# Attention layer 0: which engine reads which score bank, one mask add for three tiles, and the maxima cut into three bf16 parts before they are transposed

## The chip, the cores and the metric

One core of one Trainium2 chip runs the whole program. The metric is device time in microseconds (us) of one execution. Engines by their names in the profile: PE (matmul; PEld is its weight load), DVE (vector), ACT (scalar), POOL (GpSimd) and SP, whose queue issues DMAs. Each engine takes its instructions in order.

## The reference

Five layers follow one another: a grouped-query cross attention (layer 0), an RWKV block, a second attention, its feed-forward, and another RWKV block. The change is in layer 0 alone, which computes, for 16 batches of 100 rows against 361 context rows:

```python
q = hidden_state @ Wq + bq
k = encoder_hidden_state @ Wk + bk
v = encoder_hidden_state @ Wv + bv
...
scores = jnp.einsum('bkgld,bksd->bkgls', q, k) * scale
scores = scores + encoder_attention_mask[:, :, None, :, :]
attn = jax.nn.softmax(scores, axis=-1)
out = jnp.einsum('bkgls,bksd->bkgld', attn, v)
out = out.transpose(0, 3, 1, 2, 4).reshape(b, l, H)
out = out @ Wo + bo
x = out + hidden_state
mu = jnp.mean(x, axis=-1, keepdims=True)
var = jnp.var(x, axis=-1, keepdims=True)
return (x - mu) * jax.lax.rsqrt(var + EPS) * gamma + beta
```

There are 8 key heads of 16 channels, and 4 query heads for each.

## The kernel before, in words

Layer 0 is `layer0` (L352). Its loop (L699) goes over 32 halves `h`: batch `b = h // 2`, and `par = h % 2` says which 4 of the 8 key heads. I call a half with `par` 1 odd, one with `par` 0 even. The work of a half is set in seven slots by `order` (L698): m0, m1, w0, m2, w1, m3, w2. An "m" slot computes **maxima** (L482) of the half that comes next, a "w" slot **weights** (L526) of the present one.

- `maxima(h, q)`: four matmuls, one per head, each on 32 rows of PE, write scores (100 rows x 361 keys) into four PSUM banks; DVE adds the mask and reduces each bank to one column of `nms`, which holds minus the maximum of each row. After the fourth group (m3) DVE copies these columns twice beside themselves (L499).
- `turn_maxima(h)` (L501), at the end of slot 0: PE transposes `nms` into one bank; ACT copies it as bf16 (`high`). At slot 1 `part()` goes on: DVE forms `rest` (rows of the maxima less `high`), ACT the bf16 `mid` of it, POOL adds both into the bf16 tile `parted`. So `parted` holds three bf16 parts of each maximum, in three neighbouring rows.
- `weights(fill, h, j, slot)`: for one of three key blocks of 121 keys, four matmuls make turned scores (121 keys x 400) in four banks (r = 0 to 3), and four bf16 matmuls with `both` add the three parts of the maxima to them. Then the banks are emptied into `pt`: for j = 0, ACT copies r = 0, 1 and DVE adds the mask into r = 2, 3 as it reads them; for j = 1, 2, ACT copies three and DVE reads r = 3. POOL adds the mask to each tile that ACT copied, one instruction for each. The exponentials are put off: the tiles of DVE one slot, those of ACT `far` slots (2, 3, 3).

Score banks come from one ring of six (`score`, L356), handed out in turn: a group takes four, the transposes one. The matmuls of a group run in the order r = 3, 2, 1, 0 (`BURST`, L28). A group therefore starts with the banks that the group before it had as its second and first.

Between these, PE does **filler pieces** (`Filler`, L103): queries, keys, values, `attend` (L567, the product with the values; three per half), `divide` (L596) and `output` (L619, four pieces `o`). Each piece has a cost and a first slot. In each slot the filler gets a share, a ninth of the cost of all pieces in the list, and takes the first piece in the list that may run, until the share is spent; what is left or overdrawn goes on to the next slot. Pieces of one chain stay together, and after a chain is closed no other chain starts in that slot. The attends of a half are due at slots 5, 8 and 10, where 7 and more are slots of the next half. `divide` of a batch is due in slot 5 of the next batch's even half; its result is `s`, DVE takes reciprocals, and in slot 4 of the odd half POOL multiplies `y` by them, after which the four `o` pieces go to the end of the list, due from slot 5. Batches 0, 4 and 8 have two queries pieces to place in the odd half, batches 1, 2, 5, 6, 9 and 10 one, the others none. After `o` come DVE's residual `res`, statistics (POOL `ve`, `rstd`), then POOL `shift`, ACT `res` and POOL's last two products.

All helpers record as L89 (vector, scalar, gpsimd), L94 (matmul) or L97 (transpose), so groups are told apart by tiles. PE's order is the order of the program.

## Time and profile before

| what | value |
|---|---|
| median of 3 runs | 3151.25 us (3147.79 to 3153.27) |
| the profiled execution | 3151.7 us, span 3149.8 us |
| granted PE clock, mean | 0.960 |
| layer 0, in the span | from 0 to about 698.6 us |
| busy from 30 to 620 us (590 us) | PE 499.9, DVE 397.9, POOL 369.5, ACT 345.0 |
| the same, a batch without queries (576.2 to 613.9) | PE 32.0, DVE 26.8, POOL 26.0, ACT 23.4 of 37.7 |
| POOL mask add, 121x400 | 256 times, mean 1034 ns |
| ACT copy of a score bank, 121x400 | 256 times, mean 499 ns |
| DVE maxima reduce, 100x361 | 512 times, mean 533 ns |
| DVE mask add, 121x400 | 560 ns |
| DVE `rest`, ACT `mid`, POOL `parted`, 128x400 | 626, 628, 942 ns |

The times come from runs without the profiler; the span is what the profiler saw of one execution, from first to last instruction. In a timeline line the columns are start in us, duration in us, engine, source line, operation, written tile and read tiles, shape, count; in brackets the idle time of the engine just before, and what ended it. A float32 matmul counts as two instructions there. A matmul's end is modelled, so PE's busy time is an upper view of its work.

### The profile page before, as it was taken

The page shows a single profiled execution, that of the slowest core. Times are in us where ns is not written, and L with a number is a line of the kernel's source. Part 1 is how long each engine was busy: PE and PEld are TensorE (multiplying, and loading weights), DVE is VectorE, ACT ScalarE, POOL GpSimd, SP SyncE. Part 2 cuts the span into 40 slices and gives each one's busy share as a digit, 9 for nine tenths or more (in the row PEclk, how much of TensorE's full clock was granted, in tenths as well). Part 3 has the DMA queues.
Part 4 walks back from the last instruction along what each step waited for, and adds up shares of the span by engine and source line. Part 5 has one row for each costly group of instructions (what it writes and reads, how often), then busy time and mean ns, then how long its engine had stood idle before and what let it go on. Part 6 is the DMA issues. An engine that isn't in the chain of part 4 may idle for free. (4 is left out here: it accounts for less than half of the span.)

```text
span 3149.8 us, 43449 instructions
## 1 busy us (share of the span) xinstructions
PE 2819.1 (89%) x16083; PEld 1375.6 (44%) x16083; DVE 1752.6 (56%) x3603; ACT 1237.6 (39%) x2249; POOL 1491.1 (47%) x1291
## 2 busy tenths in 40 slices
PE   6888888858889999989999999989999788989998
PEld 3333333314344444445454555445554344444444
DVE  4676767742989989523434333331000379898981
ACT  2565566643344355422223232221111335344553
POOL 1666666663777777512222111130000367777871
PEclk9999999979899999989999999999999889999999
DMA  6010101004224253130000001020002223324321
GB/s 195 15 43 14 36 21 37 10 19 123 70 80 133 83 162 108 52 106 21 20 21 21 21 21 34 28 70 11 11 11 60 96 69 110 102 76 150 109 61 56
DMA packets 139559, 195.90 MB, mean 62 GB/s; under 512 B 23974, under 2 KB 106854, under 8 KB 139346
## 3 DMA queue, kind: packets, MB, share of 16 engines
q1 hardware_dynamic: 116306, 160.34, 17.1%
q10 hardware_dynamic: 23040, 32.78, 2.9%
q8 instruction: 127, 2.08, 0.3%
q14 instruction: 86, 0.70, 0.1%
HBM read 117.16 MB, written 49.15 MB: 53 GB/s over the span
## 5 line engine op out<-in xcount | busy, mean ns | idle before, releaser
L89 POOL TENSOR_TENSOR a<-a,rc 128x800 f32<-128x800 f32 x256 | 487.5, 1907 | 180.5 <-DVE a L89 124.7
L89 DVE TENSOR_TENSOR_SCAN a<-wc,vb 128x400 f32<-128x400 f32 x512 | 477.4, 974 | 29.4 <-PE acc L94 3.2
L89 DVE CUSTOM_DVE_ANT_0 l_junk<-l_sc,mask 100x361 f32<-100x361 f32 x512 | 273.1, 533 | 163.2 <-PE l_sc L94 104.9
L89 POOL TENSOR_TENSOR pt<-pt,maskT 121x400 f32<-121x400 f32 x256 | 258.0, 1034 | 117.4 <-ACT pt L89 117.4
L89 DVE TENSOR_TENSOR vb<-vb,kc 128x792 f32<-128x792 f32 x256 | 253.8, 991 | 8.8
L1690 DVE CUSTOM_DVE_ANT_0 junk<-l2a_sc,mask 100x361 f32<-100x361 f32 x256 | 136.9, 535 | 182.6 <-PE l2a_sc L94 164.3
L1726 POOL TENSOR_TENSOR pa<-pt,pt 121x1600 f32<-121x1600 f32 x16 | 57.1, 3570 | 364.1 <-ACT pt L1721 364.1
L94 PE MATMUL vb<-xc,sel 128*128 128x400 f32 x512 | 206.9, 487 | 20.3 <-DVE a L89 20.1
L89 POOL TENSOR_TENSOR xj<-tm,ext 128x400 f32<-128x400 f32 x160 | 153.6, 981 | 79.8 <-DVE tm L89 68.3
L1911 DVE TENSOR_TENSOR x<-pb,x 100x512 f32<-100x512 f32 x16 | 12.6, 790 | 320.1 <-DMA pb<-po 310.8
L94 PE MATMUL v<-l_v_w,ct 128*121 128x512 f32 x384 | 177.2, 605 | 0.0
L75 PE MATMUL h<-yTb,l_fc 128*128 128x400 f32 x512 | 172.8, 499 | 0.6 <-ACT yTb L343 0.6
L94 PE MATMUL k<-ct,l_k_w 128*128 128x361 f32 x512 | 170.6, 476 | 0.0
L75 PE MATMUL p<-l_proj,h 128*128 128x512 f32 x384 | 165.4, 592 | 0.0
L89 ACT ACTIVATE pt<-pt 121x400 f32<-121x400 f32 (+1 forms) x192 | 160.1, 880 | 1.0 <-POOL pt L89 0.8
L89 ACT COPY pt<-l_sc 121x400 f32<-121x400 f32 x256 | 110.4, 499 | 108.9 <-PE l_sc L94 108.9
L94 PEld LDWEIGHTS vb<-xc,sel 128*128 128x128 f32 x512 | 97.1, 198 | 113.0 <-DVE a L89 38.1
L94 PE MATMUL l_sc<-kz,qz 32*100 32x361 f32 x1024 | 112.2, 507 | 32.1 <-DVE nms L89 27.1
L75 PEld LDWEIGHTS h<-yTb,l_fc 128*128 128x128 f32 x512 | 96.9, 190 | 74.3 <-ACT yTb L343 2.5
L1721 ACT ACTIVATE pt<-l2a_sc,kmask 121x400 f32<-121x400 f32 x192 | 98.2, 594 | 65.4 <-PE l2a_sc L94 65.4
L94 PEld LDWEIGHTS k<-ct,l_k_w 128*128 128x128 f32 x512 | 93.2, 189 | 64.0 <-issue 14.5
L89 ACT ACT_TABLE_LOAD x66 | 84.7, 1283 | 91.3 <-PE mm L94 65.7
(324 smaller groups left out, 5310.6 us busy)
## 6 DMA issues: line engine op xcount, KB each, us to landing
ct<-in_ctxT SPq DMA_DIRECT2D x32, 722.0 KB
dk<-k ACTq DMA_DIRECT2D x32, 200.0 KB
kc<-dk SPq DMA_DIRECT2D x32, 200.0 KB
dv<-v ACTq DMA_DIRECT2D x32, 200.0 KB
dhi<-hi ACTq DMA_DIRECT2D x32, 200.0 KB
dlo<-lo SPq DMA_DIRECT2D x32, 200.0 KB
vc<-dv SPq DMA_DIRECT2D x32, 200.0 KB
dw<-wd ACTq DMA_DIRECT2D x32, 200.0 KB
```

Source lines behind the costliest of these rows:

```text
L75: nc.tensor.matmul(out=ps, lhsT=lhs(c), rhs=rhs(c), start=(c == 0), stop=(c == n - 1))
L89: return lambda *args, **kw: tc.keep_in_program_order(op(*args, **kw))
L94: pin(nc.tensor.matmul(**kw))
L1690: nc.vector.tensor_tensor_reduce(out=junk, in0=ss[r][:L, :S2], in1=t["mask"], scale=-1.0, scalar=FLT_MAX, op0=ALU.add, op1=ALU.min, accum_ ...
L1721: nc.scalar.activation(pt[:, r, :], st[r][:KW, :T], AF.Exp, bias=t["kmask"][:, j : j + 1], scale=1.0)
L1726: nc.gpsimd.tensor_tensor(t["pa"], t["pt"][0], pt, ALU.add)
L1911: nc.vector.tensor_tensor(x, pb[:, i, :], x, ALU.add)
```

## The change

In `layer0`:

- `weights`: for every j DVE adds the mask as it reads bank r = 0, ACT copies r = 1, 2, 3, and POOL adds the mask to these three tiles in one instruction of 121x1200. The exponential of DVE's tile is put off one slot, that of the three tiles three slots.
- the attend of j = 0 is due at slot 6 in place of 5.
- the maxima are cut into bf16 parts on POOL, right after m3's reduces and before the transposes: twice a copy into the bf16 tile `cut`, a subtraction into the next column, and a copy back, six instructions on 100x16 elements. `turn_maxima` is then four transposes and one ACT copy into `parted`; `part()`, with `rest`, `mid` and POOL's add, is gone, as are the two column copies on DVE.
- in the setup, `both` is built by one reduce per parity, and `less01` and `low01` are gone.

```diff
--- before.py
+++ after.py
@@ -365,19 +365,15 @@
             rows = one.tile([L, 3, E], F32, name="l0_rows")
 
             par01 = one.tile([128, 2], F32, name="l0_par")
-            less01 = one.tile([128, 2], F32, name="l0_less")
-            low01 = one.tile([128, 2], F32, name="l0_low")
             both = one.tile([128, 2, KW], BF16, name="l0_both")
-            mv0 = one.tile([128, 2], F32, name="l0_pair")
+            mv0 = one.tile([128, 1], F32, name="l0_three")
             bqs = one.tile([128, 4], F32, name="l0_bqs")
             kb = one.tile([128, 2], F32, name="l0_kb")
             swap = one.tile([128, 128], F32, name="l0_swap")
             junk = one.tile([L, S2], F32, name="l0_junk")
             vzs = [one.tile([KW, 3, 2, 128], F32, name=f"vz{i}") for i in range(2)]
             nms = [one.tile([L, 4, 128], F32, name=f"nms{i}") for i in range(2)]
-            high = one.tile([128, T], BF16, name="l0_high")
-            mid = one.tile([128, T], BF16, name="l0_mid")
-            rest = one.tile([128, T], F32, name="l0_rest")
+            cut = one.tile([L, 4, 4], BF16, name="l0_cut")
             parted = [one.tile([128, T], BF16, name=f"parted{i}") for i in range(2)]
 
             live, qzs, xTs = {}, {}, {}
@@ -496,7 +492,10 @@
                     )
                 if q == 3:
                     n = nms[par].rearrange("p q (r two s) -> p two s q r", two=2, s=16)[:, 1 - par]
-                    vector.tensor_copy(n[:, 1:3], n[:, 0:1].to_broadcast([L, 2, 4, 4]))
+                    for k in range(2):
+                        gpsimd.tensor_copy(cut, n[:, k])
+                        gpsimd.tensor_tensor(n[:, k + 1], n[:, k], cut, ALU.subtract)
+                        gpsimd.tensor_copy(n[:, k], cut)
 
             def turn_maxima(h):
 
@@ -504,16 +503,7 @@
                 ps = score()
                 for q in range(4):
                     turn(ps[:, q * L : (q + 1) * L], nms[par][:, q, :], ident[:L, :L])
-                scalar.copy(high, ps[:, :T])
-
-                def part():
-                    vector.scalar_tensor_tensor(
-                        rest, high, less01[:, par : par + 1], ps[:, :T], ALU.mult, ALU.add
-                    )
-                    scalar.activation(mid, rest, AF.Identity, scale=low01[:, par : par + 1])
-                    gpsimd.tensor_tensor(parted[par], rest, mid, ALU.add)
-
-                return part
+                scalar.copy(parted[par], ps[:, :T])
 
             def turn_mask(b):
                 ps = score()
@@ -541,28 +531,23 @@
                     start=False,
                 )
                 pt = t["pt", par]
-                far = (2, 3, 3)[j]
-
-                def masked(engine, dst, src, n):
-                    m = t["maskT"][:, j, None, :].to_broadcast([KW, 4 * n, L])
-                    engine.tensor_tensor(dst, src, m, ALU.add)
-
-                def parts(ap):
-                    return ap.rearrange("p (q t) -> p q t", t=L)
-
-                for r in range(far):
+                m = t["maskT"][:, j, :]
+                vector.tensor_tensor(
+                    pt[:, j, 0, :].rearrange("p (q t) -> p q t", t=L),
+                    ss[0][:KW, :T].rearrange("p (q t) -> p q t", t=L),
+                    m[:, None, :].to_broadcast([KW, 4, L]), ALU.add,
+                )
+                for r in range(1, 4):
                     scalar.copy(pt[:, j, r, :], ss[r][:KW, :T])
-                for r in range(far, 4):
-                    masked(vector, parts(pt[:, j, r, :]), parts(ss[r][:KW, :T]), 1)
-                for r in range(far):
-                    masked(gpsimd, parts(pt[:, j, r, :]), parts(pt[:, j, r, :]), 1)
+                three = pt[:, j, 1:4, :].rearrange("p r (q t) -> p (r q) t", t=L)
+                gpsimd.tensor_tensor(three, three, m[:, None, :].to_broadcast([KW, 12, L]), ALU.add)
 
                 def exp(lo, hi):
                     e = pt[:, j, lo:hi, :].rearrange("p r t -> p (r t)")
                     scalar.activation(e, e, AF.Exp)
 
-                fill.later.append((slot + 1, lambda: exp(far, 4)))
-                fill.later.append((slot + far, lambda: exp(0, far)))
+                fill.later.append((slot + 1, lambda: exp(0, 1)))
+                fill.later.append((slot + 3, lambda: exp(1, 4)))
 
             def attend(fill, b, par, j, slot):
                 n = KEYS[j][1]
@@ -662,17 +647,10 @@
             vector.tensor_reduce(par01, h8, AX.X, ALU.add)
             vector.tensor_scalar(bqs, bq, 0.25, None, ALU.mult)
             vector.tensor_scalar(kb, par01, bk, None, ALU.mult)
-            first = ident.rearrange("p (r two s) -> p two s r", two=2, s=16)
+            starts = ident.rearrange("p (r two s) -> p two s r", two=2, s=16)
             for par in range(2):
-                less, low, pair = less01[:, par : par + 1], low01[:, par : par + 1], mv0[:, par : par + 1]
-                vector.tensor_reduce(pair, first[:, 1 - par, 0, :], AX.X, ALU.add)
-                vector.tensor_reduce(less, first[:, 1 - par, 1, :], AX.X, ALU.add)
-                vector.tensor_reduce(low, first[:, 1 - par, 2, :], AX.X, ALU.add)
-                vector.tensor_tensor(less, less, low, ALU.add)
-                vector.tensor_tensor(pair, pair, less, ALU.add)
-                vector.tensor_copy(both[:, par, :], pair.to_broadcast([128, KW]))
-            vector.tensor_scalar(less01, less01, -1.0, None, ALU.mult)
-            vector.tensor_scalar(low01, low01, -1.0, None, ALU.mult)
+                vector.tensor_reduce(mv0, starts[:, 1 - par, 0:3, :], AX.XY, ALU.add)
+                vector.tensor_copy(both[:, par, :], mv0.to_broadcast([128, KW]))
             halves = ident.rearrange("p (r two s) -> p two r s", two=2, s=16)
             turned = swap.rearrange("p (r two s) -> p two r s", two=2, s=16)
             for par in range(2):
@@ -704,7 +682,7 @@
                     elif b + 1 < B:
                         values(fill, b + 1)
                     if h > 0:
-                        for j, slot in enumerate((5, 8, 10)):
+                        for j, slot in enumerate((6, 8, 10)):
                             attend(fill, b, 1, j, slot)
                         divide(fill, b, 12)
                     if h > 0 and b % G < 3 and b // G + 1 < NG:
@@ -719,20 +697,18 @@
                         gpsimd.tensor_tensor(xb[b], xb[b], rows[:, 0, :], ALU.add)
                     if b + 1 < B:
                         keys(fill, b + 1)
-                    for j, slot in enumerate((5, 8, 10)):
+                    for j, slot in enumerate((6, 8, 10)):
                         attend(fill, b, 0, j, slot)
                 share = fill.total() / 9
                 due = 0.0
                 for slot, (what, i) in enumerate(order):
-                    if slot == 1 and h >= 0:
-                        part()
                     if what == "m" and h + 1 < 2 * B:
                         maxima(h + 1, i)
                     if what == "w" and h >= 0:
                         weights(fill, h, i, slot)
                     due = fill.run(slot, due + share)
                     if slot == 0 and h >= 0:
-                        part = turn_maxima(h)
+                        turn_maxima(h)
                     if slot == 3 and par and b + 1 < B:
                         turn_mask(b + 1)
                 fill.carry(7)
```

## Prediction

> **What bounds the kernel now.** The change touches only the first of five layers, so I first ask how long that layer runs and whether its end is waited for. The slices of the page (78.7 us each) are coarse; the timeline around 690 us gives the hand-over:

> ```profile
> 697.37 1.26 POOL L89 TENSOR_TENSOR x<-res,l_rows 100x512 f32<-100x512 f32 x1
> 698.66 1.52 ACT L89 ACTIVATE xn_a<-x,fshift,frstd 100x512 f32<-100x512 f32 x2 [2.72 <-POOL x L89]
> 698.66 1.00 DVE L89 TENSOR_SCALAR xn_a<-x,fmv,frstd 100x512 f32<-100x512 f32 x2 [5.10 <-POOL x L89]
> ```

> The last line of layer 0 is POOL's `x`, and ACT and DVE of the next layer start at 698.66, when it ends. So a microsecond in layer 0 is a microsecond of the span. Inside the layer the waits of the matmul engine (PE) from 30 to 651 us are read (total us, times, longest):

> ```profile
> PE l_sc L94 <- DVE nms L89: 49.4, 60, 3.2
> PE acc L94 <- ACT pt L89: 16.9, 49, 0.6
> PE k L94 <- DVE res L89: 11.5, 13, 1.2
> PE l_sc L94 <- ACT pt L89: 2.8, 6, 1.0
> PE o L94 <- POOL y L89: 2.0, 6, 0.3
> ```

> PE is busy 499.9 of the 590 us from 30 to 620, DVE 397.9, POOL 369.5, ACT 345.0. PE runs its hand-written order, and what it loses are short waits for a PSUM bank or a tile. One row speaks to the first part of the change: PE waited for ACT to empty a score bank for 2.8 us in all. Then the order of PE's work in the half that begins at 577.50 (batch 13, a batch without `queries` pieces), from its last maxima (slot 5) to the next half's first, and POOL beside it:

> ```profile
> 592.05 0.87 PE L94 MATMUL l_sc<-kz,qz 32*100 32x361 f32 x8
> 593.21 0.88 PE L94 MATMUL acc<-pt,vz 121*32 121x400 f32 x8 [0.29 <-ACT pt L89]
> 594.29 0.95 PE L94 MATMUL l_sc<-qz,kz 32*121 32x400 f32 x8 [0.20 <-DVE nms L89]
> 595.06 0.35 PE L94 MATMUL l_sc<-parted,l_both 32*121 32x400 bf16 x4
> 595.74 1.10 PE L94 MATMUL o<-l_wo,y 128*100 128x512 f32 x2 [0.33 <-POOL y L89]
> 596.77 0.87 PE L94 MATMUL l_sc<-kz,qz 32*100 32x361 f32 x8
> ...
> 591.68 3.02 POOL L89 TENSOR_TENSOR pt<-pt,maskT 121x400 f32<-121x400 f32 x3 [2.88 <-ACT pt L89]
> 594.65 1.03 POOL L89 TENSOR_TENSOR y<-y,s 128x400 f32<-128x400 f32 x1
> 596.05 3.01 POOL L89 TENSOR_TENSOR pt<-pt,maskT 121x400 f32<-121x400 f32 x3 [0.36 <-ACT pt L89]
> ```

> Reader's point: the first output piece `o` already waits 0.33 us for POOL's `y`, though an attend (`acc`) and a weights group stand before it.

> **The change, part by part.** The sum is made against the profiled execution: 3151.7 us, span 3149.8; the median shown is 3151.25, so the two agree to 0.5 us.

> (a) *Work counts.* ACT: 32 more copies (w0 now copies three banks; 499 ns each) and 32 `mid` fewer (628 ns): nothing net. DVE: 32 masked adds (560), 32 `rest` (626) and 32 small copies (211) fewer, some 45 us of a queue that is not full. POOL: 32 `parted` (942) fewer; 96 merged masks in place of 256 single ones; 192 split instructions more. No row has a 1200-wide POOL add: between 800 (1907 ns) and 1600 (3570) it comes to 2.74 us, against 3.0 for three singles. No row has the split either (100x16): the nearest are COPY 128x16, 211 ns, TENSOR_TENSOR 100x4, 201, and the start-to-start distance of two dependent small ones, 0.28 (`shift` at 579.14 and 579.42). Six at 0.28 make 1.7 us; bounds are 6 x 0.2 = 1.2 and, if each took half of the 100x512 form, 6 x 0.63 = 3.8. I take 1.7, the rows nearest in width. No DMA moves. The setup loses a few 0.15 us DVE instructions beside the first key projections: nothing.

> (b) *Bank one to DVE.* A group's first two banks are wanted by the next group but PE waits for ACT there 2.8 us in all, nearly all of it in the first batch, which has no output pieces between its groups. Worth 1 us (bounds 0 and 2.8).

> (c) *`rest` leaves DVE.* In the even half PE's w0 waits for DVE (0.74 us at 602.22), because `rest` (600.50 to 601.05) holds back the reduces of the maxima before. Without it the second reduce ends as long after its matmuls' start as at 604.35, where w1 follows at 606.45: 2.10 us. From 599.80 that is 601.90: a gain of 0.32 per batch, 15 batches, 4.8 us. It is at most 0.74 x 15 = 11.

> (d) *The split stands in POOL's queue ahead of w2's mask.* It waits for the last reduce and takes 1.7 us. Behind it are the mask, then `shift`, then ACT's `res`, and behind `res` on ACT the exponentials that PE's next attend wants:

> ```profile
> 576.16 3.02 POOL L89 TENSOR_TENSOR pt<-pt,maskT 121x400 f32<-121x400 f32 x3 [0.28 <-ACT pt L89]
> 579.14 0.19 POOL L89 TENSOR_TENSOR shift<-mv,rstd 100x1 f32<-100x1 f32 x1
> 579.67 0.81 ACT L89 ACTIVATE res<-res,shift,rstd 100x512 f32<-100x512 f32 x1 [2.80 <-POOL shift L89]
> 580.39 1.61 ACT L89 ACTIVATE pt<-pt 121x1200 f32<-121x1200 f32 x2
> ```

> The last reduce ends at 575.6; split to 577.5; mask to 580.2; everything after it about 1.0 later. The attend in the odd half's slot 1 goes from 581.73 to 582.7. In a batch without queries the wait of w0 for DVE (0.92 at 622.22) covers it: +0.1. In a batch with queries two or three `v` pieces follow and w0 has no wait (470.29): +1.0. The transposes themselves have cover: PE waits 1.43 us for DVE right after them, so a split of up to some 3.9 us does not show there.

> (e) *Three ACT copies in w0, not two*, put 0.43 us before the exponential that slot 3's attend waits for: 0.43 in odd halves with one query, covered by the waits of w1 elsewhere.

> (f) *The first attend moves from slot 5 to slot 6.* In even halves PE already takes it in slot 6: no change. In odd halves I worked the filler's list by hand. Without queries the pieces are five attends at 0.8, three `v` at 0.9 and a divide at 0.7: 7.4 / 9 = 0.82 a slot; slot 5 has 0.62 left and today takes the attend. Afterwards the attend may not run there, and the only piece that may is the first `o` (due from slot 5). PE then stands behind w1's mask and `y` on POOL. The merged mask begins after the third copy (592.4), ends at 595.2, `y` at 596.2; PE has been free since 593.0. So `o` 596.3 to 597.3, w2 to 598.4, attend to 599.2, and the next maxima at 599.2 in place of 596.77: +2.4. Batches 3, 7, 11, 12, 13 and 14: six.
> With one query (1, 2, 5, 6, 9, 10) slot 5 takes a second query piece, slot 6 the attend and, with 0.03 of its share left, `o`, whose `y` is ready by then. PE's 0.30 wait at the attend goes, one `o` is pulled forward.

> Sum per batch: no query 0.1 + 2.4 - 0.3 = +2.2, six times 13. One query: 1.0 + 0.43 - 0.3 (attend) - 0.3 (c), about +0.7 once the pulled `o` is counted: 4. Two queries (4, 8): 1.0 - 0.3 - 0.3 = +0.4: 1. First batch -1. The tail (from 651 us) loses 0.9 by the attend that now follows the divide of 650.34, gains 0.9 because w0 no longer waits 1.62 for `parted`, and loses 0.6 by the merged masks: +0.6. Total 13 + 4 + 1 - 1 + 0.6 = **+17.6**, so 3151.7 + 17.6, about **3169 us**. Bounds: split 1.2 us, the stall of (f) at 1.7 and (c) at twice its worth give +5; split 3.8 us adds about 2 at the attend in 14 odd halves less the 0.9 that is covered in six: +17.6 + 22 = +40 at the far end.

> [...]

> **The rivals.**
> 1. *The banks were the bound.* If every wait of PE for DVE outside the two fixed ones (1.43 us after the transposes, a chain of three reduces, 14 times: 20 us) went with the lighter DVE queue, 49.4 - 20 = 29 us would go; half of it is a fair price: 3137. For it: the largest wait row names DVE. Against it: after most maxima PE waits for reduces that follow their own matmuls, which no lighter queue shortens.
> 2. *All hidden.* Losses of (d) and (f) are taken up by later waits, as PE idles 5.5 us in each batch without queries: 3151 +/- 5. It holds if the stalled DVE and ACT have work whose results PE wants next; I find none, since after the late maxima every chain starts from PE. That "bank one" does nothing by itself, (b), is the part of this that I believe.
> 3. *POOL is the bound.* If the split takes 3.8 us or POOL's queue runs late all through the half, the attends slip by 2 us more in each odd half: 3185 to 3191. It decides from a split of some 2.5 us on. For: POOL is already 63% busy here; against: the small rows.

> **How the numbers follow.** Forecast 0.73; rival 1 0.08, rival 2 0.09, rival 3 0.10. Time 3169, its own range 3159 to 3179. With rival 3's lower half and most of rival 2: 3153 to 3186. A measurement can tell 0.2% (6 us) from nothing: faster 0.08, same 0.09, slower 0.83.

> **What would show it.** In the profile after: PE `o` waiting for POOL `y` some 3 us in six odd halves, in place of 0.33; the odd half's first `acc` waiting about 1.5 us for ACT, not 0.55; w0 of the even half waiting some 0.4 and not 0.74; six split instructions of 0.2 us on POOL between w1's and w2's masks; one POOL mask of 2.7 us per group. The forecast is wrong if `o` is not ahead of the last weights group in those batches, if `y` no longer stands behind w1's mask, or if the split lasts over 2.5 us.

## The result, and the profile after

| | median us (lowest to highest) | runs |
|---|---|---|
| before | 3149.59 (3147.79 to 3153.27) | 4 |
| after | 3179.89 (3173.02 to 3181.90) | 4 |
| ratio, 95% interval | 1.0091 (1.0072 to 1.0110) | |

The change costs 0.9%: by the interval 23 to 35 us, against 17.6 forecast. The profiled run took 3173.02 us (span 3171.2), the fastest of the four and 21.3 more than that of before. By stages: layer 0 ends at 716.5 instead of 698.6 (+17.9); layer 1, counted up to the first scores of the next layer's attention, takes 6.3 us more; the rest takes 2.7 less (1707.3 against 1710.0).

First the waits of PE in layer 0 after (30 to 680 us; total us, times, longest):

```profile
PE l_sc L94 <- DVE nms L89: 37.6, 42, 3.1
PE o L94 <- POOL y L89: 19.8, 6, 3.3
PE acc L94 <- ACT pt L89: 14.7, 14, 4.1
PE k L94 <- DVE res L89: 7.5, 13, 0.7
PE l_sc L94 <- ACT pt L89: 0.6, 1, 0.6
```

The second row is the new one: six waits of 3.3 us for POOL's `y`, where before had 0.33 or 0.34 in the same six places. The last row shows that PE waits less for ACT to free a bank (2.8 before, 0.6 now). The largest wait, for DVE's `nms`, lost 12 us (49.4 before); not all of that need be the lighter DVE queue, since due5 below, which lacks the six stalls, has 41.8. Here is one of the six, in batch 13's odd half, from the fourth maxima (m3) to the next half's first (PE's timeline after):

```profile
600.49 0.87 PE L94 MATMUL l_sc<-kz,qz 32*100 32x361 f32 x8
604.67 1.26 PE L94 MATMUL o<-l_wo,y 128*100 128x512 f32 x2 [3.31 <-POOL y L89]
605.86 1.71 PE L94 MATMUL l_sc<-qz,kz 32*121 32x400 f32 x8
607.34 0.56 PE L94 MATMUL l_sc<-parted,l_both 32*121 32x400 bf16 x4
607.83 1.38 PE L94 MATMUL acc<-pt,vz 121*32 121x400 f32 x8
609.14 0.87 PE L94 MATMUL l_sc<-kz,qz 32*100 32x361 f32 x8
```

The order is the predicted one: `o` first, then w2, then the attend. But the durations, the second number of a line, are new. The same w2 took 0.95 us before, its `parted` matmuls 0.35 and the attend 0.88; here 1.71, 0.56 and 1.38. The stretches of after around this place, each as long as the shortest piece of half clock (below), tell why (stretch in us, length, busy us of PE, PEld, DVE, ACT, POOL with counts, granted PE clock, DMA share, GB/s):

```profile
598.65:602.07 3.42, 2.71 (x28) 1.39 (x24) 2.67 (x7) 3.28 (x8) 1.19 (x2) 1.00 0.00 0
602.07:605.48 3.41, 0.81 (x2) 0.25 (x2) 1.62 (x6) 0.71 (x2) 3.20 (x6) 1.00 0.00 0
605.48:608.90 3.42, 3.42 (x21) 0.94 (x20) 0.57 (x1) 0.97 (x3) 0.58 (x3) 0.50 0.00 0
608.90:612.31 3.41, 3.41 (x24) 1.46 (x24) 1.93 (x7) 1.87 (x4) 3.02 (x2) 1.00 0.03 7
```

PE is busy for only 0.81 us of the second stretch, at full clock, and the third, with w2 and the attend, is granted half the clock. In all the traces the clock record knows two values, 1.0 and 0.5, and between 60 and 650 us the 0.5 lies in pieces of 3.41 or 6.83 us. After five of the six stalls w2 takes 1.18 to 1.71 us; after the one at 521.8 it keeps its 0.95.

POOL one batch later in after, where `y` is late:

```profile
641.74 2.73 POOL L89 TENSOR_TENSOR pt<-pt,maskT 121x1200 f32<-121x1200 f32 x1 [2.22 <-ACT pt L89]
644.42 1.04 POOL L89 TENSOR_TENSOR y<-y,s 128x400 f32<-128x400 f32 x1
645.39 0.22 POOL L89 CAST l_cut<-nms 100x16 bf16<-100x16 f32 x1
645.69 0.23 POOL L89 TENSOR_TENSOR nms<-nms,l_cut 100x16 f32<-100x16 f32 x1
645.98 0.21 POOL L89 CAST nms<-l_cut 100x16 f32<-100x16 bf16 x1
```

The merged mask lasts 2.73 us (2.74 predicted), the split comes at 0.27 to 0.30 from start to start (0.28 predicted).

### The profile page after: what moved, and what is told of

It is laid out like the page before. It is cut to its first block, busy times and chain, and to the rows that moved or that the text cites. A ratio compares the mean times of both kernels' runs of the same rounds, so it can differ in the third digit from the quotient of the medians.

```text
span 3171.2 us, 43319 instructions
## 1 busy us (share of the span) xinstructions
PE 2851.7 (90%) x16083; PEld 1381.7 (44%) x16083; DVE 1716.1 (54%) x3497; ACT 1231.8 (39%) x2249; POOL 1506.2 (47%) x1291
## 3 DMA queue, kind: packets, MB, share of 16 engines
q1 hardware_dynamic: 116306, 160.34, 17.1%
## 5 line engine op out<-in xcount | busy, mean ns | idle before, releaser
L89 POOL TENSOR_TENSOR a<-a,rc 128x800 f32<-128x800 f32 x256 | 488.2, 1910 | 178.1 <-DVE a L89 116.7
L89 DVE TENSOR_TENSOR_SCAN a<-wc,vb 128x400 f32<-128x400 f32 x512 | 477.2, 973 | 28.1 <-DVE vb L89 2.0
L89 DVE CUSTOM_DVE_ANT_0 l_junk<-l_sc,mask 100x361 f32<-100x361 f32 x512 | 273.8, 535 | 181.0 <-PE l_sc L94 131.7
L89 POOL TENSOR_TENSOR pt<-pt,maskT 121x1200 f32<-121x1200 f32 x96 | 262.7, 2737 | 178.8 <-ACT pt L89 178.8
L89 DVE TENSOR_TENSOR vb<-vb,kc 128x792 f32<-128x792 f32 x256 | 253.7, 991 | 8.8
L94 PE MATMUL vb<-xc,sel 128*128 128x400 f32 x512 | 208.8, 491 | 18.6 <-DVE a L89 18.3
L89 POOL TENSOR_TENSOR xj<-tm,ext 128x400 f32<-128x400 f32 x160 | 154.2, 987 | 84.0 <-DVE tm L89 74.4
L94 PE MATMUL v<-l_v_w,ct 128*121 128x512 f32 x384 | 177.2, 605 | 0.0
L89 ACT COPY pt<-l_sc 121x400 f32<-121x400 f32 x288 | 123.1, 501 | 133.9 <-PE l_sc L94 133.2
L94 PE MATMUL k<-ct,l_k_w 128*128 128x361 f32 x512 | 170.6, 476 | 0.0
L89 ACT ACTIVATE pt<-pt 121x400 f32<-121x400 f32 x192 | 159.1, 884 | 1.3 <-POOL pt L89 1.3
L94 PEld LDWEIGHTS vb<-xc,sel 128*128 128x128 f32 x512 | 97.5, 198 | 110.8 <-issue 39.3
L94 PE MATMUL l_sc<-kz,qz 32*100 32x361 f32 x1024 | 113.2, 510 | 26.4 <-DVE nms L89 25.8
L94 PE MATMUL acc<-pt,vz 121*32 121x400 f32 (+1 forms) x768 | 119.9, 532 | 17.4 <-ACT pt L89 17.4
L94 PEld LDWEIGHTS k<-ct,l_k_w 128*128 128x128 f32 x512 | 93.2, 189 | 64.0 <-issue 14.5
```

Source lines behind the costliest of these rows:

```text
L89: return lambda *args, **kw: tc.keep_in_program_order(op(*args, **kw))
L94: pin(nc.tensor.matmul(**kw))
```

## The experiments

After the result my theory was: the due slot alone is the loss, by its stall and the half clock that follows; the rival: it is the new parts, the merged mask and the split. Later groups ask what each new part costs, and then what the half clock costs. In the table, "L0" is where the last instruction of layer 0 ends in the profiled run, and "half" how many us of half clock lie between 60 and 650 us of that run. Ratios are to the kernel before, on the same chip in the same job; the medians of before in the three jobs were 3153.66, 3155.54 and 3151.36.

| kernel | what it is | median us | ratio (95%) | L0 | half |
|---|---|---|---|---|---|
| before | | 3149.6 | 1 | 698.6 | 17 |
| after | | 3179.9 | 1.0091 (1.0072 to 1.0110) | 716.5 | 24 |
| due5 | after, due slot back at 5 in odd halves | 3157.15 | 1.0008 (0.9998 to 1.0017) | 707.2 | 10 |
| before_due6 | before, due slot 6 in odd halves | 3177.18 | 1.0070 (1.0050 to 1.0090) | 721.8 | 36 |
| warm | after, PE kept at work in the six stalls | 3166.71 | 1.0041 (1.0027 to 1.0055) | 713.5 | 17 |
| due5_dve | due5, split on DVE | 3166.71 | 1.0030 (1.0017 to 1.0043) | 713.1 | 7 |
| after_again | after, once more | 3178.49 | 1.0079 (1.0061 to 1.0096) | 727.7 | 48 |
| weights_only | before, new weights alone | 3162.89 | 1.0022 (1.0013 to 1.0032) | 707.8 | 3 |
| split_pool | before, split alone | 3181.77 | 1.0085 (1.0066 to 1.0104) | 726.6 | 61 |
| split_dve | split_pool, split on DVE | 3183.59 | 1.0091 (1.0070 to 1.0111) | 738.3 | 55 |
| busy_before | before, one idle matmul per odd half | 3150.08 | 1.0000 (0.9987 to 1.0014) | 699.5 | 3 |
| busy_split_pool | split_pool, the same matmul | 3161.81 | 1.0039 (1.0022 to 1.0056) | 716.6 | 37 |
| busy_after | warm, the same matmul | 3163.82 | 1.0042 (1.0021 to 1.0063) | 709.2 | 0 |

(For before_due6 three runs from 3169.83 to 3182.62 are given; a fourth of 11045.86 us isn't in the ratio.)

**The due slot, taken back (due5).**

```diff
-                        for j, slot in enumerate((6, 8, 10)):
+                        for j, slot in enumerate((5, 8, 10)):
```

in the odd half's list alone.

> The changed kernel with the odd half's first attend due at slot 5 again, all else kept. Theory (the six odd halves without queries lose about 3.4 us each, 2.4 by the order and 1 by PE at half clock after the 3.3 us wait): PE's wait of o for POOL y falls from 19.8 us to under 3, layer 0 ends near 697 us in place of 716.5, and the time comes to 3151 +/- 5. Rival (the split on POOL and the third ACT copy are the cost): at least 3165.

The time came as the theory had it: level with before. PE's wait for `y` in layer 0 is down to this row of due5:

```profile
PE o L94 <- POOL y L89: 3.2, 7, 1.1
```

Layer 0 itself ended later than it should have: 8.5 us after before's, of which later layers of that profile gave back 6.4. So the other parts aren't free inside the layer.

**The due slot alone (before_due6).** The same edit the other way round, on before.

> The kernel before with one number changed: the odd half's first attend due at slot 6. Theory: o waits for y some 2.8 us in six odd halves (y ends 0.5 earlier here, with single masks), 1.8 us lost by the order each and up to 1 by the half clock: 3150 + 11 to 17, so 3161 to 3167. Rival (the due slot alone is harmless; it takes the merged masks and the split): 3148 to 3153.

This one number costs 0.7%, more than the theory's own sum. Batch 11's odd half in before_due6 shows the stall without any new mask or split, and the half clock behind it:

```profile
524.95 2.03 PE L94 MATMUL o<-l_wo,y 128*100 128x512 f32 x2 [2.82 <-POOL y L89]
526.91 1.66 PE L94 MATMUL l_sc<-qz,kz 32*121 32x400 f32 x8
```

The stall is 2.82, but `o` takes 2.03 instead of 1.10 and w2 1.66 instead of 0.95: 1.6 us lost behind the wait, on top of it. The odd halves without queries last 23.0 us where the clock holds and 25.0, once 26.0, where it doesn't (before: 19.9 to 21.3). The rival, that the new parts are the loss, falls as a full account.

**The stall kept, the clock held (warm).** In the six halves three matmuls whose result is overwritten stand before the first `o`:

```diff
                     t = bank(f"o0_{b}")
+                    if b + 2 < B and ((b + 1) % G == 3 or b + 1 >= 12):
+                        for _ in range(3):
+                            mm(out=t[:L, :], lhsT=ident[:, :L], rhs=wo[:, 0, :], start=True, stop=True)
```

> The changed kernel with three matmuls of 100x512 that nothing reads, issued in the bank of o while PE waits for y in the six odd halves without queries. Theory (a wait of 3.3 us lets the clock fall, and w2 and the attend after it then run at half speed): w2 after o takes 0.95 us again, not 1.71, and 1.1 us a half is won: layer 0 ends near 710, about 3173 against the changed kernel's 3180. Rival (the slow matmuls have another cause, or the extra ones delay o): layer 0 ends at 716 or later.

Batch 3's odd half in warm:

```profile
201.00 2.82 PE L94 MATMUL o<-l_wo,ident 128*100 128x512 f32 x6
204.35 1.10 PE L94 MATMUL o<-l_wo,y 128*100 128x512 f32 x2 [0.54 <-POOL y L89]
205.38 0.95 PE L94 MATMUL l_sc<-qz,kz 32*121 32x400 f32 x8
206.43 0.88 PE L94 MATMUL acc<-pt,vz 121*32 121x400 f32 x8
```

`o` is as late as in after, but w2 and the attend run at full clock, in all six halves. The ratio falls from 1.0091 and 1.0079 (after, measured twice) to 1.0041, intervals apart: some 12 to 16 us, or 2 to 2.6 for each stall, without `o` coming sooner. The profiled layer 0 ends 3.0 us before the first profile of after and 14.1 before the second; their half clock was 24 and 48 us, against 17 here.

**The split on DVE (due5_dve).** In due5, the six small instructions go from `gpsimd` to `vector`, to see whether POOL's queue is what the split costs.

> As due5, with the six split instructions on DVE in place of POOL. Theory (the split holds up POOL's w2 mask and through shift and ACT's res the next odd half's first attend by 1 us, which shows in the eight odd halves with queries): the first acc's group in these halves ends 1 us sooner, 4 to 8 us won against due5, about 3145. Rival (that delay is hidden, and 1.2 us more on DVE holds banks): equal to due5 or slower.

It was slower, not faster. DVE in due5_dve, and POOL beside it:

```profile
657.76 0.17 DVE L89 CAST l_cut<-nms 100x16 bf16<-100x16 f32 x1
657.97 2.74 DVE L89 TENSOR_TENSOR nms<-nms,l_cut 100x16 f32<-100x16 f32 x1
...
657.95 2.71 POOL L89 TENSOR_TENSOR pt<-pt,maskT 121x1200 f32<-121x1200 f32 x1 [0.70 <-ACT pt L89]
```

A subtraction of 100x16 lasts 2.74 us; POOL's mask began 0.02 us before it and ended 0.05 us before it. This is the one of 64 that lasts so (median 187 ns), but PE then waits 5.10 us for DVE's `res`, and this half lasts 20.96 us in place of due5's 15.36: 5.6 of the 5.9 us by which layer 0 ends later than there. Whether every execution has it isn't known.

**The same kernel again (after_again).**

> The changed kernel as it is, beside the three that follow on one chip. It should repeat 1.007 to 1.011 of the kernel before.

The ratio repeats, but this profile has twice the half clock of the first (48 us, 24) and layer 0 ends 11.2 later. So layer 0's +17.9 in the first profile was the lower of two draws; this one has +29.0.

**The new weights alone (weights_only).** The hunk of `weights` in the change, put on before: banks, merged mask, exponentials; not the due slot, not the split.

> The kernel before with the new emptying of the score banks alone (DVE reads bank one, ACT three, one mask instruction on POOL, exponentials at one and three slots); the maxima's chain and the due slots as before. Theory (bank one is worth nothing, the merged mask that waits for the third copy and the third copy in w0 put 1.0 us on odd halves with queries, nine of them): 3 to 10 us slower than before, layer 0 ends at 702 to 708, odd halves with one query take 22.3 us or more in place of 21.3, even halves the same 17.4. Rival (banks freed sooner are worth something): not slower.

As the theory said. In the odd half's slot 1 the mask on POOL can only start after the third copy, and the attend's last matmuls end 2.9 us after the maxima's start instead of 2.3. PE in weights_only:

```profile
472.98 0.87 PE L94 MATMUL l_sc<-kz,qz 32*100 32x361 f32 x8 [1.32 <-DVE nms L89]
473.77 0.86 PE L94 MATMUL acc<-pt,vz 121*32 121x400 f32 x2
475.02 0.87 PE L94 MATMUL acc<-pt,vz 121*32 121x400 f32 x6 [0.38 <-ACT pt L89]
```

The attend is cut in two: a quarter of it (r = 0, DVE's tile, exponentiated early) runs at once, the rest waits. That breaks PE's idle stretch, and this profile has only 3 us of half clock (17 before).

**The split alone (split_pool, split_dve).** The hunks of `maxima`, `turn_maxima` and the setup on before, with `part()` gone; then with the six instructions on `vector`.

> The kernel before with the maxima split on POOL ahead of the transposes and one ACT copy after them, the emptying of banks and the due slots as before. Theory (rest no longer holds up DVE: 0.3 to 0.5 us an even half, 15 of them; the split in front of w2's masks costs 1 us in the eight odd halves with queries): the even halves take 17.0, the odd with one query 22.3, layer 0 ends within 4 us of 699. Rival (the split on POOL is the costly part): layer 0 ends at 705 or later.

> As split_pool, with the six split instructions on DVE. Theory (nothing stands in front of w2's masks now): even halves 17.0 and odd ones 21.3, layer 0 ends 4 to 8 us sooner than before, about 3145. Rival (DVE's instructions with two inputs in SBUF wait for POOL's masks, as one of 2.74 us did, and hold up the reduces or res): no gain against split_pool.

Both of my sizes for split_pool were far too small: alone, the split costs nearly as much as the whole change. Batch 9's odd half in split_pool:

```profile
441.06 1.32 PE L94 MATMUL l_sc<-kz,qz 32*100 32x361 f32 x8 [1.53 <-DVE nms L89]
443.40 1.56 PE L94 MATMUL acc<-pt,vz 121*32 121x400 f32 x8 [1.02 <-ACT pt L89]
444.88 3.60 PE L94 MATMUL v<-l_wv,ct 128*121 128x128 f32 x16
448.41 0.95 PE L94 MATMUL l_sc<-qz,kz 32*121 32x400 f32 x8
```

The wait for ACT is only 1.02 us, but it follows one of 1.53, and the work after them runs slow: `acc` 1.56 for 0.88, two `v` pieces 3.60 where after has 2.01 for them. 61 of 590 us are at half clock. The even halves are shorter as forecast (mostly 17.1 us, before 17.4); the loss is in the odd ones. On DVE the split is no better: its median copy back is 564 ns instead of some 180. All 75 split instructions that last over 0.3 us there end 0.03 to 0.05 us after a POOL instruction, 70 of them after a mask, as the one of 2.74 us did; and the transposes come later.

**What the half clock costs (the busy three).** One matmul, whose result is overwritten by the transposes, stands ahead of them in odd halves and shortens PE's idle stretch:

```diff
                 ps = score()
+                if par and 0 < h < 2 * B - 1:
+                    mm(out=ps[:, :512], lhsT=ident, rhs=wo[:, 0, :], start=True, stop=True)
```

> The kernel before with the same extra matmul. Theory: its 17 us of half clock go, layer 0 ends at 690 to 694, 4 to 8 us faster than before (ratio 0.997 to 0.999), so faster than both kernels. Rival: the extra work costs PE as much as it saves, same or slower.

> split_pool with one extra matmul of 128x512 that nothing reads, in the transposes' bank ahead of them, in the odd halves, where PE waits 1.5 us for DVE anyway. Theory (split_pool is slow by PE's half clock, which some 60 us of its stretch from 60 to 650 us show against 17 before, each costing 0.4 us; the clock falls where PE idles about half of a 3.4 us window, and the extra matmul breaks that idle stretch): hardly any half clock is left, layer 0 ends at 701 to 707 in place of 726.6, and 20 us or more of the time go. Rival (the split's place in POOL's queue costs the time by itself, the clock only follows): layer 0 ends past 718.

> The changed kernel with that extra matmul and with the three of the run warm. Theory: no half clock is left from 60 to 650 us; what remains is the order alone, layer 0 ends near 706, the time is 10 to 15 us over before (ratio 1.003 to 1.005). Rival: if the order costs less than thought, under 1.002.

In busy_before the half clock goes from 17 to 3 us and the time stays; I was wrong to expect a gain. The two profiles show both sides: batches 2 to 14 take 4.2 us less (501.0 against 505.1), 3.2 of it in batches 6 and 8, which had half clock, but batch 2 begins 5.5 us later. Of these, 2.6 come ahead of the first transposes, where no extra matmul has run yet, and 2.0 in batch 1, which has the remaining piece of half clock. How much of that the extra matmul causes isn't shown. In split_pool the same matmul gains about 14 us (ratio 1.0085 to 1.0039) although it adds work. Layer 0 ends at 716.6, where I expected 701 to 707, since 37 us of half clock are left: the wait of `acc` behind it is untouched.

```profile
475.02 1.13 PE L94 MATMUL l_sc<-l_wo,ident 128*128 128x512 f32 x2
477.11 0.87 PE L94 MATMUL l_sc<-kz,qz 32*100 32x361 f32 x8 [0.62 <-DVE nms L89]
479.46 0.95 PE L94 MATMUL acc<-pt,vz 121*32 121x400 f32 x8 [1.48 <-ACT pt L89]
480.34 3.56 PE L94 MATMUL v<-l_wv,ct 128*121 128x128 f32 x16
```

busy_after has no half clock at all in the 590 us. Beside busy_before it shows what the change costs without it, which the next part uses. No version tried beats before; due5 and busy_before are level with it.

## Why the prediction was right in sign and short in size

*The mechanism of (f) was right.* Six stalls of 3.29 to 3.31 us in the six odd halves named, `o` ahead of w2; taken away (due5), the loss goes, and put alone on before (before_due6), it comes. Rival 3's condition falls (the split takes 1.7 us in after, though without the new weights it was dear all the same: split_pool), rival 2 falls with the result, and so does rival 1: 12 us less waiting for DVE at the scores came with a layer that is 17.9 us longer. Nor were the small steps wrong: w0 of the even half waits 0.46 us (0.4 predicted), and with single masks, in before_due6, the stall is 2.82 and not 3.30, the 0.5 us by which the expectation of before_due6 had `y` end sooner there.

*The size failed at (f)'s price.* The sum's "the next maxima at 599.2 in place of 596.77: +2.4" prices a stall by the wait and the new order alone, and takes every piece behind it at its old duration. The granted clock wasn't in the sum. It could have been: before's own tail has the pattern, 2.79 us of idle and then an attend of 1.56 instead of 0.88 and a w2 of 1.71 instead of 0.95:

```profile
658.08 1.56 PE L94 MATMUL acc<-pt,vz 119*32 119x400 f32 x8 [2.79 <-ACT pt L89]
659.57 1.71 PE L94 MATMUL l_sc<-qz,kz 32*121 32x400 f32 x8
```

Where the clock falls behind such a stall, the half lasts some 1.6 us more: in after 23.1 us where it holds, which is 2.3 over before's 20.8 and so what (f) said, and 24.7 in three halves where it doesn't (27.5 in batch 12's, where it falls twice).

*Without the half clock the sum was some 4 us too high.* Beside each other, busy_before and busy_after give layer 0 +9.7 us (699.5 to 709.2), but their medians differ by 13.7 (3150.08 and 3163.82). The 9.7 is a low draw: busy_after's profiled run is the fastest of its seven, and busy_before's layer 0 began late, with the first transposes at 58.1 us (55.2 to 57.4 in the other profiles). Up to batch 2's transposes busy_after is 5.7 us ahead, where after is 1.8 ahead of before; from there to the end of the layer it takes 15.5 more. So the work costs about 14 us, against 17.6 forecast. By parts of the 9.7, lengths taken from transposes to transposes:

| part | predicted | busy pair |
|---|---|---|
| odd halves, no queries (6) | +2.5 each: 15 | +2.3 each: 13.9 |
| odd halves, one query (6) | about +1.1 each: 6.8 | 6.6 in all |
| odd halves, two queries (2) | +0.7 each: 1.4 | 2.1 |
| even halves (15) | -0.32 each, (c): -4.8 | -13.2, of it -3.0 in batches 0 and 1 |
| up to the first transposes (predicted for the first batch) | -1 | -2.6 |
| tail after the last transposes | +0.6 | +2.9 |

The odd halves without queries are as predicted (batch 0's, which isn't in the table, is 0.1 shorter, and the last even half 0.2 longer). The even halves gain more than (c): -0.3 to -0.4 is the common case, but after a half with one queries piece it is -1.2 to -1.6, because one `o` (1.0 us) has moved out of it into the odd half before, while the prediction counted it at 0.1 net. That makes the agreement of the odd halves with one query luck: the `o` is in their 6.6 us, and without it they lose at most 0.5 each, not 1.1. From such an odd half to the end of the next even one, batches 2 to 10 come to -0.2 or +0.3 us, where the sum has about +0.7. So (d) and (e) were mis-sized there: the first attend does end 0.6 to 1.1 later, but little of that is left at the end of the half; the waits for ACT's `pt` from 30 to 651 us went from 49 (16.9 us) to 13 (10.6). The tail was mis-sized, since (f) acts there too, and twice the wait is longer than before's 2.79 and 2.17. After:

```profile
674.36 1.55 PE L94 MATMUL acc<-pt,vz 119*32 119x400 f32 x6 [4.08 <-ACT pt L89]
683.03 3.73 PE L94 MATMUL o<-l_wo,y 128*100 128x512 f32 x4 [5.15 <-POOL y L89]
```

On top of the work stands the half clock: layer 0 ends 7.3 us later than busy_after's in after's profile (24 us of half clock) and 18.5 in after_again's (48 us), 0.3 to 0.4 us for each; the ratios (1.0091 and 1.0079 beside 1.0042) make it 12 to 15. So a forecast with both right would have been about 14 for the work and 12 to 15 for the clock; mine got as near as it did partly by luck, because too high a work term stood in for some of the clock that it lacked.

*(d) was put down to one part alone.* The odd half's first attend mostly ends 3.4 us after the maxima's start, as predicted (2.3 + 1.0), though with a wait of 0.9 and not 1.5 us, since a quarter of it runs ahead. But the split without the merged mask gives 3.3 and the merged mask without the split 2.9: they overlap, and either alone has most of the effect. The times overlap even more: alone the new weights cost 0.22% and the split 0.85%, together (due5) 0.08%. After, slot 1 of an odd half:

```profile
467.17 0.87 PE L94 MATMUL l_sc<-kz,qz 32*100 32x361 f32 x8 [1.42 <-DVE nms L89]
467.96 0.86 PE L94 MATMUL acc<-pt,vz 121*32 121x400 f32 x2
469.71 0.87 PE L94 MATMUL acc<-pt,vz 121*32 121x400 f32 x6 [0.89 <-ACT pt L89]
470.51 2.01 PE L94 MATMUL v<-l_wv,ct 128*121 128x128 f32 x16
```

DVE's early tile seems to be what protects after here: the split's delay is the same as in split_pool, but `acc` x2 stands in the middle of it and `v` keeps its clock. That early start as the reason for the kept clock is read from the traces; no run put the old banks' order under the new split with nothing else changed.

*Open.* Layer 1, counted as above, lasts 741.2 us in before's profile and 747.4 to 747.6 in after, after_again and warm, but 741.3 in busy_after, though its instructions are the same in all of them; over all profiles it goes from 741.0 to 747.6, and the last layer, from its first `xn_a`, from 692.6 to 703.4. What sets this wasn't tried, and 6 us of the measured loss may lie there.

## What to carry to other kernels

Moving one piece's earliest slot changes which piece is taken in its place: look up what that piece waits for, because in an engine that runs in order everything behind it waits too (in after `o` stood 3.3 us for `y`, and w2 and the attend behind it). Price a stall of the matmul engine by its length and by the durations of what runs after it, taken from rows after a stall of like length in the same trace; equal stalls can end differently (w2 took 1.18 to 1.71 us behind five of after's stalls of 3.3 us, 0.95 behind the sixth), so expect a spread. And ready work put into an idle stretch can be a gain although it adds to the engine's work: one matmul of 1.13 us in each odd half took split_pool from 1.0085 to 1.0039; the same matmul on before, which had 17 us of half clock, left the time as it was (1.0000).

## What the runs showed of the hardware

```profile
437.93:441.34 3.41, 1.88 (x20) 0.90 (x20) 1.82 (x7) 0.00 (x0) 3.32 (x6) 1.00 0.06 23
441.34:444.75 3.41, 2.39 (x16) 0.20 (x8) 2.58 (x11) 3.10 (x5) 2.40 (x3) 0.50 0.00 0
516.74:520.15 3.41, 1.76 (x16) 1.04 (x16) 2.63 (x7) 3.19 (x7) 2.11 (x1) 1.00 0.33 76
520.15:523.57 3.42, 1.76 (x10) 0.70 (x14) 0.77 (x4) 0.00 (x0) 2.84 (x8) 1.00 0.40 145
```

The stall of 3.31 us that fell mostly into one window left it 0.81 us of work (602.07), and the clock fell; the one of 3.30 us that the grid cut in the middle left 1.76 in each, and the clock held. Over the thirteen profiles these are 2179 windows at full clock. The 75 that were followed by half clock had PE busy for 0.16 to 0.55 of their length, the other 2104 for 0.48 or more. Of 95 windows at half clock, the 20 that were followed by another had 0.87 or less, the 75 that were followed by full clock 0.88 or more. So in this layer about half a window of idle time could be enough for the clock to be lost, it came back only behind windows with work in 0.88 or more of them, and none of the 75 windows behind which it was lost was wholly idle. In after alone the six of these windows had 0.20 to 0.48, all others at full clock 0.51 or more.

A small DVE instruction can last as long as a POOL instruction: a subtraction with two inputs 2.74 us for 0.19 in due5_dve, beside a mask of 2.71 us, and copies with one input up to 1.18 us for 0.18 in split_dve. The ratio of due5_dve beside that of due5 (1.0030 and 1.0008) makes POOL, not DVE, the better place for the split beside masks of this length.
